# Edge ordering by source in a four-layer graph network: one of three scaled one-hots made on VectorE instead of ScalarE

## The chip, the core and the metric

The kernel runs on one core of a Trainium2 chip. A core has TensorE (PE in the profile; PEld is its weight load), VectorE (DVE), ScalarE (ACT), GpSimd (POOL) and SyncE (SP), each with an instruction queue of its own that is worked off in order; queues wait for each other through semaphores. The metric is the device time of one execution in microseconds, the median of several runs.

## What is computed

The input is a graph of 6250 nodes with 256 features each and 100000 edges (src, dst), sorted by dst. Four graph layers follow one another, each with a residual and a layer norm:

```python
edge_index = jnp.stack([src, dst])
x = _layernorm(x + _L0_gnn_ref(x, edge_index, ...))       # mean of relu(layernorm(x)) over the edges, two matrices
x = _layernorm(x + _L1_gnn_ref(x, src, dst, ...))         # attention with 8 heads: queries at src, keys and values at dst
x = _layernorm(x + _L2_gnn_ref(x, edge_index, ...))       # two graph attention layers with 4 heads
x = _layernorm(x + _L3_gnn_ref(x, edge_index, ...))       # mean of x over the edges, three matrices
```

Layers 0, 2 and 3 sum over the edges of each dst, for which the edges come in order. Layer 1 sums over the edges of each src (`segment_sum(..., row)` with `row = src`), so the kernel must order the edges by source first:

```python
s = jnp.einsum('ehd,ehd->eh', q[row], k[col])
m = jax.ops.segment_max(s, row, num_segments=n)
p = jnp.exp(s - m[row])
denom = jax.ops.segment_sum(p, row, num_segments=n)
out = jax.ops.segment_sum((p / denom[row])[:, :, None] * v[col], row, num_segments=n)
```

## The kernel before

**Blocks and pieces.** The nodes lie in 50 blocks of 125. Each block has 16 chunks of 128 edges of its own, and ten blocks share 2 more chunks for what doesn't fit. A layer's pass goes over *pieces*: in layer 0, three pieces a block with 6, 6 and 4 chunks, 150 in all (numbered 0 to 149 in the prediction). A piece (`piece0`, L1659) gathers its rows from a table in HBM with one indirect DMA per chunk, issued by POOL (`gather`, L926, L927), into a tile of which there are four buffers; makes the one-hot of its keys on DVE (`one_hots`, L936, three buffers); and adds the rows to the block's sum on PE (`add_rows`, L995). After a block's last piece `finish0` (L1613) does the layer's dense part: the mean (L1620), transposes, products with w_l and w_r (`product`, L923), residual and norm (L1638, L1639, L882 to L893), then the products for layer 1's k, v and q (L1646, L1650, L1652) and the stores to kv_table and q_table on SP's queue.

**Ordering by source beside it.** `by_source` (L1341) runs beside layer 0. It is a generator that yields the cost of each step, and `beside` (L1685) hands out about 7.3 us of it per piece. It first finds for each edge its block and its place in the block (`lo`, the place modulo 128; `col`, the chunk and block). The edges lie as 125 rows by 800 columns. For each column `c` (the loop at L1513) it then makes `oh` (L1518), the one-hot of `col` over a window of chunks and blocks, and `o1` (L1520), the one-hot of `lo` over the 128 places, both on DVE in 16-bit form; scales `o1` per row by two parts of the edge's value, `oa` (L1522) and `ob` (L1524), on ACT; and adds the products of `oa` and `ob` with `oh` to an accumulator in PSUM (L1529). All 800 columns add to the same accumulator. For the columns whose window reaches the last block (`w1 == NC`, columns 600 to 799) there is a third scaled one-hot, `oc`, the places times the block's number plus one (`val_c`, L1491), which is multiplied with the last ten columns of `oh` (L1535): it tells for the shared chunks which block each edge belongs to. `oh` has four buffers, `o1`, `oa`, `ob` and `oc` three each. After the last column the accumulator is closed (L1539) and decoded on DVE (L1542 to L1570) to the lists by source: `idx_s`, `key_s`, and `idx_1` (L1570), the list for the first chunks of blocks 0 and 1.

**Layer 1.** The first eight chunks of blocks 0 and 1, 16 gathers in all, are taken from the first rows of kv_table with `idx_1` (L1813, L1814), before the whole table is there. All other gathers (L1816) wait for the last row of kv_table, which block 49's `finish0` writes.

**What sets the order.** The program is recorded piece by piece, and a scheduler then lays the instructions of each engine's queue in an order by its own estimate of what is ready when. A change of one instruction's engine so moves others too, on all queues, the gathers of POOL among them.

Of the kernel before, what the change touches and what calls it, by code (L numbers as in the profile page):

```python
# [11 lines left out]
AF = mybir.ActivationFunctionType  # L12
ALU = mybir.AluOpType
# [3 lines left out]
P = 128  # L17
# [638 lines left out]
def gnn_stack_kernel(ctx: ExitStack, tc: tile.TileContext, ins, out):  # L656
# [13 lines left out]
    nc = tc.nc  # L670
# [21 lines left out]
    EQ, NG = EP, 8  # L692
# [47 lines left out]
    with ExitStack() as fast:  # L740
# [600 lines left out]
        def by_source(pool, work, psum):  # L1341
# [131 lines left out]
            lo, col = place, ups[1].rearrange("p g q -> p (g q)")  # L1473
# [16 lines left out]
            val_c = ups[0].rearrange("p g q -> p (g q)")  # L1490
# [9 lines left out]
            iota_h = pool.tile([P, NC], F16, name="iota_h")  # L1500
# [12 lines left out]
            for c in range(EC):  # L1513
                at = slice(c, c + 1)
                w0, w1 = wide[c]
                n = w1 - w0
                oh = work.tile([EQ, WIDE], F16, name="oh", bufs=4)
                nc.vector.tensor_scalar(oh[:, :n], iota_h[:EQ, w0:w1], col[:, at], None, op0=ALU.is_equal)  # L1518
                o1 = work.tile([EQ, P], F16, name="o1", bufs=3)
                nc.vector.tensor_scalar(o1, iota_h[:EQ, :P], lo[:, at], None, op0=ALU.is_equal)  # L1520
                oa = work.tile([EQ, P], F16, name="oa", bufs=3)
                nc.scalar.activation(oa, o1, AF.Copy, scale=val_a[:, at])  # L1522
                ob = work.tile([EQ, P], BF16, name="ob", bufs=3)
                nc.scalar.activation(ob, o1, AF.Copy, scale=val_b[:, at])  # L1524
                for o in (oa, ob):
                    for k, (c0, c1) in enumerate(banks):
                        e0, e1 = max(c0, w0), min(c1, w1)
                        if e0 < e1:
                            nc.tensor.matmul(  # L1529
                                acc[:, k, e0 - c0 : e1 - c0], o, oh[:, e0 - w0 : e1 - w0], start=False, stop=False  # L1530
                            )
                if w1 == NC:
                    oc = work.tile([EQ, P], F16, name="oc", bufs=3)
                    nc.scalar.activation(oc, o1, AF.Copy, scale=val_c[:, at])
                    nc.tensor.matmul(of_block, oc, oh[:, NM - w0 : n], start=False, stop=False)  # L1535
                if c % 4 == 3:
                    yield 3.6
# [27 lines left out]
            for o, v, n in ((idx_s, low[:, :NM], CM), (far_s, low[:, NM:], SH)):  # L1565
                nc.vector.tensor_scalar(
                    o.rearrange("p b c -> p c b"), v.rearrange("p (c b) -> p c b", c=n), float(N - 1), 0.0,
                    op0=ALU.min, op1=ALU.max,
# [20 lines left out]
        with tc.tile_pool(name="f0", bufs=1) as pool, tc.tile_pool(name="f0w", bufs=2) as work, tc.tile_pool(  # L1589
# [9 lines left out]
            scale = (D // 8) ** -0.5  # L1599
# [59 lines left out]
            def piece0(b, c0, n):  # L1659
# [15 lines left out]
                if last:  # L1675
                    add_rows(sums[b], st[:, n:, :], gs, CM, SH, 1)
                    yield
                    yield from finish0(b)

            work_s = by_source(spool, swork, psum)  # L1680
            work_d = shared_by_target(psum)

# [394 lines left out]
        with tc.tile_pool(name="f3", bufs=1) as pool, tc.tile_pool(name="f3w", bufs=2) as work, tc.tile_pool(  # L2077
            name="f3g", bufs=5
        ) as gp, tc.tile_pool(name="f3p", bufs=1, space=bass.MemoryType.PSUM) as psum:
            iota_h = pool.tile([P, P], F16, name="iota_h3")  # L2080
# [179 lines left out]
```

## Time and profile before

| what | us |
|---|---|
| median of 4 runs | 5157.44 (5155.97 to 5160.06) |
| profiled execution | 5153.93 |
| its span | 5152.0 |
| first and last `oc` (L1534) start | 991.0 and 1212.2 |
| last gather of layer 0 starts | 1244.59 |
| first gather of layer 1 with idx_s starts | 1274.92 |

The profile is of one execution. A row of a group gives the line, engine, operation, output and inputs, shapes and count, then the busy time in us and the mean duration in ns, then the engine's idle time just before and what ended it. Neighbouring instructions of DVE and ACT overlap: what an operation costs its queue is the distance from its start to the start of the next, which is less than its duration. A row of a timeline gives start, duration, engine, line, and in brackets the idle time before and its releaser.

### The profile page before, as it was taken

The numbers are of one execution on the slowest core, as the hardware profiler recorded it, in microseconds if no ns is written. First come the engines' busy times: TensorE is split into PE (matmuls) and PEld (weight loads), VectorE is DVE, ScalarE is ACT, GpSimd is POOL, SyncE is SP. The second block draws the span as 40 slices with busy tenths as digits, with TensorE's granted clock in tenths as the row PEclk, the third lists the DMA queues.
The fourth block names the chain that finished last, engine by engine and source line by source line (L and its number), as shares of the span: only waits on it lengthen the run. The fifth ranks groups of instructions, "written<-read, shape, count | busy, mean of one in ns | idle before, by whom it ended". The sixth has DMA issues, their size and how long they took to land.

```text
span 5152.0 us, 84598 instructions
## 1 busy us (share of the span) xinstructions
PE 4245.1 (82%) x27926; PEld 3093.2 (60%) x27926; DVE 3531.3 (69%) x10485; ACT 2162.9 (42%) x6203; POOL 3770.6 (73%) x3889
## 2 busy tenths in 40 slices
PE   0467999987999999987887887877777777799997
PEld 0245667665676676665666666655655565456675
DVE  7576788766888888876666666657777777423434
ACT  4011898895344344433444444434444444211222
POOL 6677777776777777757777777767777777677776
PEclk9777999988999999998999999989889899899998
DMA  4556677666777777764444544444444444789975
GB/s 131 146 158 178 177 193 192 186 173 181 222 224 227 223 226 226 226 180 120 133 132 130 137 131 134 130 118 132 132 132 134 133 135 135 208 241 246 246 208 146
DMA packets 365012, 883.97 MB, mean 172 GB/s; under 512 B 83596, under 2 KB 181954, under 8 KB 364562
## 3 DMA queue, kind: packets, MB, share of 16 engines
q0 software_dynamic: 232032, 702.40, 49.7%
q1 hardware_dynamic: 132530, 176.06, 11.7%
q8 instruction: 222, 3.64, 0.3%
q14 instruction: 228, 1.87, 0.1%
HBM read 791.50 MB, written 86.63 MB: 170 GB/s over the span
## 4 chain that ended last, share of the span: by engine, by line
PE 33%; POOL 28%; issue 17%; DMA 12%; DVE 9%; ACT 2%; SPq 0%; DVEq 0%; POOLq 0%; ACTq 0%
POOL g L927 26%; PE ps L1846 7%; DMA g<-hs_table_f,idx_d 5%; PE ps L995 4%; PE qe L1826 4%; PE po L923 3%; PE pt L923 3%; PE d L2180 3%; PE acc L1529 3%; DMA g<-x_table_f,idx_d 2%; DMA g<-kv_table_f,idx_s 2%; DMA g<-h_table_f,idx_d 1%; DVE st L936 1%; DVE a_hot L1897 1%; DVE msg L1982 1%
## 5 line engine op out<-in xcount | busy, mean ns | idle before, releaser
L927 POOL DMA_INDIRECT g<-hs_table_f,idx_d x1600 | 1535.0, 959 | 487.4 <-issue 427.7
L927 POOL DMA_INDIRECT g<-h_table_f,idx_d x800 | 791.9, 990 | 296.3 <-issue 209.9
L2048 PE MATMUL ps<-msg,st 128*125 128x260 f32 x3200 | 898.1, 424 | 74.1 <-DVE msg L1982 52.1
L927 POOL DMA_INDIRECT g<-kv_table_f,idx_s x784 | 748.7, 955 | 250.2 <-issue 181.9
L995 PE MATMUL ps<-g,st 128*128 128x256 bf16 (+1 forms) x4032 | 640.7, 285 | 187.1 <-DMA g<-h_table_f,idx_d 88.5
L2048 PEld LDWEIGHTS ps<-msg,st 128*125 128x125 f32 x3200 | 639.5, 208 | 212.1 <-issue 50.4
L927 POOL DMA_INDIRECT g<-x_table_f,idx_d x544 | 515.8, 948 | 186.3 <-issue 152.9
L995 PEld LDWEIGHTS <-st 128*128 128x128 bf16 x4536 | 448.8, 102 | 282.7 <-issue 174.4
L1982 DVE TENSOR_TENSOR msg<-g,pp 128x1024 f32<-128x1024 f32 x400 | 484.8, 1212 | 19.3 <-ACT pp L1979 18.5
L1976 DVE TENSOR_TENSOR e<-g,pe 128x16 f32<-128x16 f32 x400 | 67.6, 169 | 578.2 <-DMA g<-hs_table_f,idx_d 405.2
L2015 PE MATMUL pe<-ad_parts,ts 125*128 125x4 bf16 x4800 | 177.9, 165 | 323.0 <-DVE e L1976 267.8
L936 DVE TENSOR_TENSOR st<-iota_p,key_d 128x500 f32<-128x500 f32 (+1 forms) x550 | 409.7, 745 | 49.2 <-PE ps L995 27.5
L2015 PEld LDWEIGHTS <-ts 125*128 125x128 bf16 x4800 | 177.4, 96 | 436.2 <-issue 333.9
L1846 PE MATMUL ps<-msg,st 128*125 128x264 f32 x1600 | 421.8, 401 | 2.5 <-DVE msg L1780 2.3
L1979 ACT ACTIVATE pp<-r 128x16 f32<-128x16 f32 (+1 forms) x410 | 76.7, 187 | 628.2 <-DVE r L1970 438.4
L948 ACT CAST ts<-tp 125x512 bf16<-125x512 f32 x400 | 230.6, 577 | 247.2 <-PE tp L946 239.6
L1522 ACT ACTIVATE oa<-o,blk 125x128 f16<-125x128 f16 x800 | 312.5, 391 | 38.8 <-PE acc L1529 27.9
L1829 DVE TENSOR_TENSOR prod<-g,qe 128x512 f32<-128x512 f32 x400 | 270.4, 682 | 79.3 <-PE qe L1826 45.6
L1826 PE MATMUL qe<-q,ts 125*128 125x256 bf16 x2400 | 319.6, 276 | 5.4 <-DMA q<-q_table_f 3.3
L1846 PEld LDWEIGHTS ps<-msg,st 128*125 128x125 f32 x1600 | 283.1, 189 | 63.8 <-ACT st_s L978 2.5
L1897 DVE TENSOR_SCALAR a_hot<-a_nodes,a_ends 128x500 f16<-128x500 f16 x950 | 319.0, 363 | 2.3 <-PE a_acc L1919 2.1
L1919 PE MATMUL a_acc<-a_hot,a_st 128*128 128x500 f16 x950 | 292.8, 400 | 30.3 <-ACT a_row L1906 21.1
(463 smaller groups left out, 8703.2 us busy)
## 6 DMA issues: line engine op xcount, KB each, us to landing
g<-hs_table_f,idx_d POOLq DMA_INDIRECT x1600
a_table_f<-a_row SPq DMA_DIRECT2D x50, 437.5 KB
cnt<-a_table_f SPq DMA_DIRECT2D x50, 437.5 KB
xs<-x_table_f SPq DMA_DIRECT2D x50, 336.0 KB
g<-h_table_f,idx_d POOLq DMA_INDIRECT x800
g<-kv_table_f,idx_s POOLq DMA_INDIRECT x784
hs_table_f<-hs SPq DMA_DIRECT2D x100, 115.5 KB
own<-hs_table_f SPq DMA_DIRECT2D x100, 115.5 KB
```

Source lines behind the costliest of these rows:

```text
L923: nc.tensor.matmul(ps, aT[:, k, :], w[:, k, :], start=(i == 0), stop=(i == n - 1))
L927: nc.gpsimd.indirect_dma_start(out=g, out_offset=None, in_=table, in_offset=bass.IndirectOffsetOnAxis(ap=idx, axis=0))
L936: nc.vector.tensor_tensor(st, iota_p[:, None, :w].to_broadcast([P, n, w]), key[:, :, None].to_broadcast([P, n, w]), op=ALU.is_equal,)
L995: nc.tensor.matmul(ps[:, :m], st[:, i, :], g[:, i, k * D : k * D + m], start=(c0 + i == 0 and k == 2), stop=(c0 + i == CH - 1 and k == 0),)
L1522: nc.scalar.activation(oa, o1, AF.Copy, scale=val_a[:, at])
L1826: nc.tensor.matmul(qe[:, i, :], ts[:, i0 + i, :], q[:, k * D : (k + 1) * D], start=(k == 0), stop=(k == 2))
L1846: nc.tensor.matmul(sums[b], hot, m[:, i * H1 : (i + 1) * H1, :].rearrange("p h c -> p (h c)"), start=(c == 0), stop=(c == CH - 1),)
L1897: nc.vector.tensor_scalar(hots[k][:, i, :], nodes[:, r * RW : (r + 1) * RW], ends[:, s, c : c + 1], None, op0=ALU.is_equal,)
L1919: nc.tensor.matmul(accs[s, r], sts[s][:, c, :], hot[:, i, :], start=(c == reach[r][0]), stop=(c == reach[r][1] - 1),)
L1982: nc.vector.tensor_mul(msg[:, : n * H2, :C2].rearrange("p (n h) c -> p n h c", h=H2), g[:, :n, :D].rearrange("p n (h c) -> p n h c", h=H2) ...
L2015: nc.tensor.matmul(pe[:, i, :], ts[:, i, :], ad_parts[:, b, k, :], start=(k == 0), stop=(k == 2))
L2048: nc.tensor.matmul(sums[b][:B, : D + H2], hot, m[:, i * H2 : (i + 1) * H2, :].rearrange("p h c -> p (h c)"), start=False, stop=(c == CH - 1),)
```

## The change

In the columns whose window reaches the last block, the rows by place times the block are no longer made by an ACTIVATE from `o1` on ScalarE. A `tensor_scalar` on VectorE makes them from the same inputs as `o1` itself, in one operation of two parts: it compares the places 0 to 127 with `lo`, and multiplies the result with `val_c`. Both are scalars per row. The values of `oc`, its shape, its type and its three buffers stay, and so does the product that reads it.

```diff
@@ -1531,7 +1531,9 @@
                             )
                 if w1 == NC:
                     oc = work.tile([EQ, P], F16, name="oc", bufs=3)
-                    nc.scalar.activation(oc, o1, AF.Copy, scale=val_c[:, at])
+                    nc.vector.tensor_scalar(
+                        oc, iota_h[:EQ, :P], lo[:, at], val_c[:, at], op0=ALU.is_equal, op1=ALU.mult
+                    )
                     nc.tensor.matmul(of_block, oc, oh[:, NM - w0 : n], start=False, stop=False)
                 if c % 4 == 3:
                     yield 3.6
```

`oc` no longer depends on `o1`. In the changed kernel as built, DVE has 200 instructions more and ACT 200 fewer; the lines behind L1534 are two higher.

## The prediction

> **What bounds the kernel now.** I read the page first (which engine is busy when), then the busy time by stretches around the changed line, the waits and groups of that stretch, the chain of waits, and last the timelines of single engines. The page has no engine at its limit over the whole span:
>
> ```profile
> PE 4245.1 (82%) x27926; PEld 3093.2 (60%) x27926; DVE 3531.3 (69%) x10485; ACT 2162.9 (42%) x6203; POOL 3770.6 (73%) x3889
> ```
>
> The changed line runs only from 991.0 to 1212.2 us: 200 times, for columns 600 to 799 of the 800, where the window reaches the last block. Busy time by stretches (start:end, length, then busy us and count of PE, PEld, DVE, ACT, POOL, then clock, DMA share, GB/s):
>
> ```profile
> 650.00:950.00 300.00, 288.42 (x2499) 216.48 (x2499) 256.35 (x1062) 264.90 (x880) 227.49 (x239) 0.99 0.70 191
> 990.00:1050.00 60.00, 49.72 (x358) 35.64 (x356) 35.90 (x132) 43.89 (x147) 45.67 (x48) 0.91 0.65 174
> 1050.00:1100.00 50.00, 46.51 (x310) 32.18 (x308) 35.02 (x136) 48.77 (x165) 37.82 (x41) 0.90 0.68 188
> 1100.00:1150.00 50.00, 45.21 (x311) 32.09 (x310) 34.98 (x136) 47.20 (x159) 34.77 (x37) 0.91 0.61 167
> 1150.00:1215.00 65.00, 59.51 (x432) 44.03 (x431) 45.73 (x175) 60.79 (x202) 38.42 (x41) 0.91 0.54 149
> ```
>
> From 1050 on ACT is 94 to 98% busy and DVE 70%: ACT sets the pace. Who waits for it, from 990 to 1215 (total us, times, longest), and the changed group there:
>
> ```profile
> DVE oh L1518 <- PE acc L1535: 42.3, 60, 2.4
> ...
> POOL g L927 <- PE acc L1529: 23.2, 15, 5.9
> DVE o L1520 <- ACT oc L1534: 11.4, 37, 0.4
> ```
> ```profile
> L1534 ACT ACTIVATE oc<-o,ups 125x128 f16<-125x128 f16 x200 | 77.7, 389 | 1.4 <-PE acc L1535 1.4
> ```
>
> DVE waits 42 us for buffers that the `oc` product on PE frees. POOL, which issues the gathers (one per 1.25 us), has four long waits for PE (4.4, 5.9, 5.0 and 4.4 us at 1134, 1160, 1185 and 1209); beyond the usual 0.3 us they come to 18.7 us. The stage ends on POOL:
>
> ```profile
> 1209.64 0.94 POOL L927 DMA_INDIRECT g<-h_table_f,idx_d  x1 [4.41 <-PE acc L1529]
> ...
> 1244.59 0.95 POOL L927 DMA_INDIRECT g<-h_table_f,idx_d  x1 [0.30 <-issue]
> ...
> 1262.34 0.95 POOL L927 DMA_INDIRECT g<-kv_table_f,idx  x1 [0.31 <-issue]
> 1274.92 1.91 POOL L927 DMA_INDIRECT g<-kv_table_f,idx_s  x1 [11.64 <-DMA kv_table_f<-kv]
> ```
>
> The last gather of layer 0 starts at 1244.59; block 49 is then finished and written to kv_table, and the gathers of layer 1 that need all of that table start at 1274.92, 30.3 us later. The 14 early kv gathers between them (1245.84 to 1263.3) cost nothing: POOL would be idle. From 1300 the next stage is 99% PE-busy and unchanged, so a shift of 1274.92 goes into the end time one for one.
>
> **The change, part by part.**
>
> *ACT loses 200 ACTIVATEs.* Back to back they start 0.29 us apart (the `oa`, `ob`, `oc` rows of its timeline), so 58 us of ACT's 220 go. What is late next is the question, not these 58 us.
>
> *DVE gains 200 two-part operations.* No row has this form at 128 elements. The nearest are starts of neighbours on DVE (start, duration):
>
> ```profile
> 1108.57 0.26 DVE L1520 TENSOR_SCALAR o<-iota_h,place 125x128 f16<-125x128 f16 x1
> 1108.75 0.28 DVE L1518 TENSOR_SCALAR oh<-iota_h,ups 125x260 f16<-125x260 f16 x1
> ```
> ```profile
> 1356.05 0.27 DVE L859 TENSOR_SCALAR ln_t<-ln_y,ln_w 125x1 f32<-125x1 f32 x1
> 1356.24 0.42 DVE L1765 TENSOR_TENSOR x_sb<-x_sb,o 125x256 f32<-125x256 f32 x1
> ```
> ```profile
> 1359.88 0.14 DVE L850 TENSOR_SCALAR ln_w<-mv 125x1 f32<-125x1 f32 x1
> 1359.94 0.67 DVE L1829 TENSOR_TENSOR prod<-g,qe 128x512 f32<-128x512 f32 x1
> ```
>
> `o` is the same data with one scalar per row: 0.16 us unhindered, 0.205 mean over the stretch. L859 takes two scalars per row: 0.19 us with one element, against 0.06 for L850, which takes none. So `oc` is about 0.19 + 0.03 = 0.22 unhindered and 0.265 with the hindrance that `o` shows; I take 0.245, nearest to both. Ends: 0.15 (the second scalar free) and 0.33 (L859 plus 128 elements at the 1.1 ns each of L805, 2304 elements in 2.54 us). At 197 in the stretch: 48 us, from 30 to 65.
>
> [...]
>
> *DVE's sum.* In the changed kernel's built order, between DVE's 600th `oh` (990.2 us in the trace) and the last column operation stand 201 `oh`, 201 `o`, 197 `oc`, 23 one-hots L936 and 8 sets of finish0's operations. Mean starts apart where nothing waited: `oh` 0.236, `o` 0.205, L936 0.867, a set 3.83. Without `oc`: 47.4 + 41.2 + 19.9 + 30.6 = 139.1. The same prices give 145.5 for the order of before, where 220.4 us less 67.6 idle is 152.8, so I add 5%: 146.1. With `oc`: 194.4 us, and the columns end at 1184.6 if DVE never waits (before: 1210.6 for the last `o`). But a pacing engine does wait: ACT, which sets the pace now, idled 22.5 of 220 us (10%); DVE as a chaser idled 15% of 650:950. The others would have room: a block with 24 columns costs DVE 16.5 + 2.6 + 3.8 = 23 us, ACT 24 x 0.58 + some 3 = 17, POOL 20, and PE, which did a block in 20 us in 650:950 with four long products a column, has two and a short one here. So I take 6%, with ends 0 and 12%: columns end at **1197** (1185 to 1211).
>
> *The order on the other queues moves with it.* The scheduler thinks the columns done sooner. On PE the 800th column now comes before the last product of piece 139 of the 150 pieces (0 to 149); before, of piece 143. On POOL, 13 of the 16 early kv gathers now stand before the last four gathers of layer 0, against 2: 11 x 1.25 = 13.75 us that were hidden in the tail and now lie ahead of the last gather. SP's queue swaps some loads of h rows with stores of q rows near the end. Its issues take 0.3 to 0.4 us and it is idle between them, so I cost that at nothing; a load held behind a store would cost some 3 us (the landing of the last q store, 1276.4 to 1280.1).
>
> *POOL's sum.* The gather tiles have 4 buffers, so piece 143 can be gathered when PE is done with piece 139, some 2.5 us after the columns end. Then 36 h gathers and 13 kv gathers follow at 1.255: the last starts 60.2 us later, at 1197 + 2.5 + 60.2 = 1259.7, that is 15.1 later than 1244.59. The kv gathers themselves need idx_1, 15 to 20 us after the columns end, and POOL reaches them 25 us after: no wait, but little cover.
>
> *The tail.* Block 49 now has block 48's twelve products right behind its last gather's, with their input ready; before, they waited for x of block 48 and held block 49's w_l product to 8.2 us after the last L995. I take 5.2, so 3 us less (0 to 6). Net at the start of layer 1: 15.1 - 3 = **+12 us**.
>
> The three `oc` that move up to 452 us are 0.7 us where DVE waits for PE: nothing, at most 0.7.
>
> The profiled execution took 5153.9 us (span 5152.0 and 1.9 around it), 3.5 below the median of 5157.4. So 5166 for it, and 5169 against the median.
>
> **The rivals.**
>
> *A: ACT's relief wins (not slower).* Speaks for it: 54 us of DVE's waits (42.3 + 11.4) are for `oc` alone. If `oc` starts 0.15 apart, the columns end at 990.2 + 175.7 = 1166; POOL is then never held. It decides at 1177 (1239.7 - 62.7, where 1239.7 is 1244.59 - 18.7 + 13.75). Gain 18.7, cost 13.75, tail 3: -8 us, 5149. Against: L859's 0.19. [...]
>
> *B: DVE paces but hardly waits.* Columns end at 1180 to 1190: -5 to +5, about 5157. For: ACT and PE lose their own backlog. Against: 15% idle of DVE in 650:950.
>
> *C: DVE waits as it does now in 650:950, and more.* 12 to 15% idle, or `oc` at 0.33: columns end at 1211 to 1219, +26 to +34; a wait for idx_1 in front of the last h gathers would add up to 8. About 5187. POOL's gathers start 1.265 us apart among the 398 `o` and `oh` of the stretch and 1.25 apart without them (1245 to 1262), 2.5 us in all, so 197 more operations add 1.2. [...]
>
> That the instruction goes elsewhere than said is excluded: the build shows 200 more TensorScalar on DVE, 200 fewer on ACT.
>
> **How the numbers follow.** My case (columns end 1191 to 1205, +6 to +20, 5163 to 5177): 0.48. B: 0.20. A: 0.12. C: 0.20. A measurement of this kernel tells some 0.2% (10.3 us) from no change. Slower by more: 0.40 of my case and all of C, 0.60. Faster by more needs A and a tail at its best: 0.07. The rest, 0.33, is within. Range: A's lower half and C's upper half left out, 5151 to 5189.
>
> **What would show it.** Right: DVE 85 to 95% busy from 1000 to 1195 with ACT near 70%; the wait of `oh` for L1535 well under 42 us; `oc` at 0.28 to 0.35 us duration; last column `o` near 1197; last h_table gather near 1260; first idx_s gather near 1287. Wrong: `oc` as short as `o`; no POOL wait for PE between 1130 and 1200 (rival A); POOL waiting in front of a kv gather with h gathers behind it (C); or a stage after 1300 that changes length.

## The result and the profile after

The changed kernel takes 5149.31 us (median of 40 runs, 5141.96 to 5156.74), the kernel before 5157.2 in the same comparison (60 runs): a ratio of 0.9984, with a 95% interval of 0.9979 to 0.9988. The forecast was 5169; the time lies just below its range (5151 to 5189), and on the other side of no change. It is the number of rival A.

The profiled execution took 5160.14 us (span 5158.3), 10.8 above the median. The excess is not in the changed stretch. Before it, column 600 starts 7.3 us later than in the trace of before (996.43 against 989.17); behind it, from the first gather of layer 1 with idx_s to its end this execution has 5160.14 - 1272.83 = 3887.3 us, the one of before 5153.93 - 1274.92 = 3879.0, and those of the experiments below 3878.5 to 3883.8. No instruction of the change lies there, so I read the trace only up to that gather.

Busy time by stretches after the change (same columns as before: stretch, length, busy us and count of PE, PEld, DVE, ACT, POOL, clock, DMA share, GB/s):

```profile
990.00:1050.00 60.00, 58.73 (x484) 42.50 (x481) 56.79 (x252) 51.12 (x166) 45.36 (x49) 1.00 0.69 189
1050.00:1100.00 50.00, 47.07 (x356) 32.15 (x355) 47.62 (x213) 41.22 (x129) 38.11 (x40) 0.97 0.67 183
1100.00:1150.00 50.00, 48.94 (x390) 34.10 (x388) 49.59 (x228) 43.95 (x142) 38.11 (x40) 1.00 0.70 188
1150.00:1215.00 65.00, 57.73 (x373) 42.27 (x372) 47.06 (x171) 27.08 (x82) 49.45 (x52) 0.89 0.69 193
```

DVE is 95 to 99% busy where it was 70%, ACT 82 to 88% where it was 94 to 98%. DVE now sets the pace of the columns, as forecast; but POOL is not slowed: 40 gathers in each 50 us, one per 1.25 us. Who waits, from 990 to 1215 (total us, times, longest):

```profile
POOL g L927 <- issue: 47.6, 156, 0.3
PEld L1529 <- ACT ob L1524: 11.7, 49, 2.5
PEld L1529 <- ACT oa L1522: 10.8, 41, 0.5
...
DVE kv L1652 <- PE po L923: 9.2, 3, 6.6
```

DVE's 42.3 us of waiting for `oh`'s buffer (the product of `oc`, now L1537) and the 11.4 us of `o` for `oc` are gone. So are POOL's four long waits: only its usual 0.3 us per gather are left. The waits of PE for `oa` and `ob` are longer than before (22.5 against 17.7 us), but nothing that ends the stage hangs on them. The groups of DVE in the stretch and, from its timeline (start, duration), one column and the start of the next:

```profile
L1534 DVE TENSOR_SCALAR oc<-iota_h,place,ups 125x128 f16<-125x128 f16 x197 | 63.0, 320 | 2.8 <-PE acc L1537 2.6
L1520 DVE TENSOR_SCALAR o<-iota_h,place 125x128 f16<-125x128 f16 x211 | 59.4, 287 | 0.4 <-ACT ob L1524 0.2
```
```profile
1102.04 0.25 DVE L1520 TENSOR_SCALAR o<-iota_h,place 125x128 f16<-125x128 f16 x1
1102.21 0.30 DVE L1534 TENSOR_SCALAR oc<-iota_h,place,ups 125x128 f16<-125x128 f16 x1
1102.43 0.28 DVE L1518 TENSOR_SCALAR oh<-iota_h,ups 125x260 f16<-125x260 f16 x1
1102.63 0.50 DVE L1520 TENSOR_SCALAR o<-iota_h,place 125x128 f16<-125x128 f16 x1
```

From start to start, `o` takes 0.17 us here, `oc` 0.22, `oh` 0.20. The stretch begins with the first `oh` that is 310 wide, that of column 600 (the row counts two), and ends with the last `oc`; in the trace of before it ends with the last `o`. First the two rows of after, then those of before:

```profile
996.43 0.56 DVE L1518 TENSOR_SCALAR oh<-iota_h,ups 125x310 f16<-125x310 f16 x2
1170.00 0.30 DVE L1534 TENSOR_SCALAR oc<-iota_h,place,ups 125x128 f16<-125x128 f16 x1
```
```profile
989.17 0.55 DVE L1518 TENSOR_SCALAR oh<-iota_h,ups 125x310 f16<-125x310 f16 x2
1210.64 0.25 DVE L1520 TENSOR_SCALAR o<-iota_h,place 125x128 f16<-125x128 f16 x1
```

POOL's timeline at the end of the stage (start, duration, in brackets the idle time before and its releaser):

```profile
1212.47 0.95 POOL L927 DMA_INDIRECT g<-kv_table_f,idx  x1 [0.30 <-issue]
...
1242.54 0.95 POOL L927 DMA_INDIRECT g<-kv_table_f,idx  x1 [0.30 <-issue]
1243.79 0.95 POOL L927 DMA_INDIRECT g<-h_table_f,idx_d  x1 [0.31 <-issue]
...
1247.55 0.94 POOL L927 DMA_INDIRECT g<-h_table_f,idx_d  x1 [0.30 <-issue]
...
1272.83 1.91 POOL L927 DMA_INDIRECT g<-kv_table_f,idx_s  x1 [20.59 <-DMA kv_table_f<-kv]
```

Thirteen early kv gathers stand ahead of the last four h gathers, without a wait, and the last h gather starts at 1247.55, 3 us *later* than before, although the columns ended 40 us sooner. By these absolute times the gain at the start of layer 1 comes from the tail, which is 25.3 us against 30.3. Counted from column 600, which started 7.3 us later, the last h gather comes 4.3 us sooner than before, and the tail is 5.1 us shorter.

The whole stage moves by some microseconds from trace to trace: column 600 starts between 989.0 and 996.4 us in the nine of this study, and single traces do not tell whether that is the execution or the kernel. I therefore count from that start. All kernels by that measure, from timelines of DVE and POOL (us; of DVE's idle time, what the timeline lists):

| kernel | columns take | of it DVE idle | POOL held by PE | column 600 to first idx_s gather | against before | median against before |
|---|---|---|---|---|---|---|
| before | 221.5 | 68.5 | 4 long waits | 285.8 | | |
| after | 173.6 | 4.7 | no | 276.4 | -9.4 | -7.9 |
| early kv gathers last, after | 171.1 | 2.9 | no | 260.7 | -25.1 | -23.0 |
| early kv gathers last, before | 220.6 | 66.1 | 4 long waits | 283.2 | -2.6 | 0.0 |
| `oc` issued twice | 223.4 | 9.0 | 9 long waits | 313.7 | +27.9 | +27.2 |
| `oc` twice in two of three columns | 208.1 | 8.8 | 5 long waits | 300.4 | +14.7 | +12.7 |
| `oc` made once | 168.0 | 26.7 | no | 269.4 | -16.4 | -13.9 |
| `oc` with one scalar | 168.0 | 8.4 | no | 273.1 | -12.7 | -12.5 |
| more buffers, before | 220.2 | 67.8 | 4 long waits | 284.5 | -1.3 | +0.2 |

The last two columns agree within 3 us in every row: what the change does to the time is done by the start of layer 1, and that start is what has to be explained. Where POOL is not held, its own count of gathers gives it: take 1.25 us off for each early kv gather that stands ahead of the last four h gathers (13, 0, 8 and 11 in these four kernels, by POOL's timelines), and 276.4, 260.7, 269.4 and 273.1 all become 259.3 to 260.7, although DVE had between 141 and 169 us of work in the columns.

### The profile page after: what moved, and what is told of

Same layout as the page of the kernel before. It is cut to its first block, busy times and chain, and to the rows that moved or that the text cites. A ratio compares the mean times of both kernels' runs of the same rounds, so it can differ in the third digit from the quotient of the medians.

```text
span 5158.3 us, 84506 instructions
## 1 busy us (share of the span) xinstructions
PE 4225.4 (82%) x27926; PEld 3077.5 (60%) x27926; DVE 3560.2 (69%) x10685; ACT 2113.7 (41%) x6003; POOL 3783.3 (73%) x3889
## 5 line engine op out<-in xcount | busy, mean ns | idle before, releaser
L995 PE MATMUL ps<-g,st 128*128 128x256 bf16 (+1 forms) x4032 | 640.9, 284 | 220.3 <-DMA g<-h_table_f,idx_d 114.7
L995 PEld LDWEIGHTS <-st 128*128 128x128 bf16 x4536 | 449.0, 101 | 321.7 <-issue 212.9
L936 DVE TENSOR_TENSOR st<-iota_p,key_d 128x500 f32<-128x500 f32 (+1 forms) x550 | 409.4, 744 | 50.7 <-PE ps L995 30.7
L1522 ACT ACTIVATE oa<-o,blk 125x128 f16<-125x128 f16 x800 | 313.3, 392 | 46.8 <-PE acc L1529 27.3
```

Of the source, the lines that this page charges most:

```text
L936: nc.vector.tensor_tensor(st, iota_p[:, None, :w].to_broadcast([P, n, w]), key[:, :, None].to_broadcast([P, n, w]), op=ALU.is_equal,)
L995: nc.tensor.matmul(ps[:, :m], st[:, i, :], g[:, i, k * D : k * D + m], start=(c0 + i == 0 and k == 2), stop=(c0 + i == CH - 1 and k == 0),)
```

## The experiments

The theory after the result: DVE's sum was too large, so that the columns end before POOL is ever held; from there on POOL's own count of gathers sets the end, and the kv gathers that moved ahead eat most of the gain. The rival theory: the columns' end still sets the time, or the moved kv gathers are hidden.

**The early kv gathers behind the last h gather.** The order of POOL alone is changed: a gather with `idx_1` may be issued only after the last gather of layer 0.

```diff
-                    gather(g[:, i, :], h_table[:, :], idx_d[:, b, c0 + i : c0 + i + 1])
+                    last_g[0] = gather(g[:, i, :], h_table[:, :], idx_d[:, b, c0 + i : c0 + i + 1])
...
-                        gather(g[:, i, :], kv_table[:ROWS, :], idx_1[:, b, c0 + i : c0 + i + 1])
+                        with tc.issue_after(last_g[0].ins):
+                            gather(g[:, i, :], kv_table[:ROWS, :], idx_1[:, b, c0 + i : c0 + i + 1])
```

> The changed kernel, with its 16 early kv gathers queued on POOL behind the last gather of layer 0 (13 of them stood in front of the last four); the order of the other engines is the changed kernel's. Theory 1 (POOL's issue rate ends layer 0 once the columns end early enough): the last h_table gather starts 13 x 1.25 = 16 us earlier against the first one's start of the stretch, the 16 kv gathers (20 us) fit into the 25 us tail behind it, and the first idx_s gather comes 11 to 16 us earlier: about 5149 - 14 = 5135, ratio 0.9957 to the kernel before (0.995 to 0.997). Theory 2 (the dense products of the last blocks on PE end layer 0): the place of the kv gathers is of no account, 5149, ratio 0.9984.

Measured: 5135.06 us (5 runs), a ratio of 0.995 with an interval of 0.9936 to 0.9963 to the kernel before (5158.07). POOL's timeline of this kernel:

```profile
1229.40 0.95 POOL L927 DMA_INDIRECT g<-h_table_f,idx_d  x1 [0.30 <-issue]
1230.65 0.94 POOL L927 DMA_INDIRECT g<-kv_table_f,idx  x1 [0.30 <-issue]
...
1249.39 0.95 POOL L927 DMA_INDIRECT g<-kv_table_f,idx  x1 [0.30 <-issue]
1255.19 1.36 POOL L927 DMA_INDIRECT g<-kv_table_f,idx_s  x1 [4.85 <-DMA kv_table_f<-kv]
```

All sixteen kv gathers now lie in the tail, where POOL would be idle (20.59 us of waiting have become 4.85), and the last h gather starts 18.15 us sooner than after the change: thirteen gathers at 1.25 are 16.25, and the stage started 1.9 sooner. So the moved gathers did cost what they were priced at. This version is faster than both kernels.

The same edit in the kernel before, where only two of these gathers stood ahead of the last four h gathers:

> The kernel before with the same edit: only two kv gathers move behind the last h_table gather. Theory 1: 2 x 1.25 = 2.5 us less at most, 5154.7, ratio 0.9995, POOL still held by PE for some 19 us between 1130 and 1210. Theory 2: no change, 1.000. Together with the run of the changed kernel it prices ScalarE against VectorE with POOL's order the same in both: theory 1 says 16 to 20 us between them, theory 2 some 8.

Measured: 5158.03 us (11 runs), a ratio of 1.000 (0.9991 to 1.0009). POOL is still held by PE (waits of 4.3 to 5.8 us), and nothing is gained; but here only two gathers could move, 2.5 us at most, which this interval does not tell from nothing. In the changed kernel thirteen moved, for 14 us. With POOL's order the same in both, `oc` on VectorE instead of ScalarE is worth 23 us (5158.0 against 5135.1), more than the 16 to 20 that were expected: most of what the change can give was hidden by the order.

**`oc` issued twice.** In every column the same operation into the same tile a second time.

```diff
+                    nc.vector.tensor_scalar(
+                        oc, iota_h[:EQ, :P], lo[:, at], val_c[:, at], op0=ALU.is_equal, op1=ALU.mult
+                    )
```

> The changed kernel with the new operation issued twice for each column. If DVE's load decides whether POOL is held (theory 1), the columns end 197 x 0.225 = 44 us later than 1170, at 1214, POOL waits for PE and for idx_1, and the end comes 30 to 42 us after the changed kernel's: 5180 to 5191, ratio 1.004 to 1.007. If DVE has room to spare (theory 3: what counts is only that ACT is relieved), the time stays within 5 us of 5149.

Measured: 5185.31 us (4 runs), 1.0056 (1.0041 to 1.0072), inside what the first theory gave. 393 operations take 87.5 us on DVE, 0.223 each from start to start, and the columns 223.4 us. PE holds POOL again, nine times for 1.3 to 6.3 us.

**`oc` made once and used for all columns** (the shared chunks' sums by block are left out by this; the products on PE stay).

```diff
-                    oc = work.tile([EQ, P], F16, name="oc", bufs=3)
+                    if c == EC - 2 * GQ:
+                        oc = pool.tile([EQ, P], F16, name="oc_once")
```

> The changed kernel with oc made for the first of its columns alone and used for all (the sums for the shared chunks' blocks are so wrong; all other work stays). DVE is rid of the 44 us. Theory 1: POOL was not held in the changed kernel either, so nothing is won but the five kv gathers that this build leaves behind the last four h_table gathers (8 ahead, against 13): 6 us, 5143, ratio 0.997. Theory 4 (DVE's new load still costs part of the gain): 5133 or less, ratio under 0.9955.

Measured: 5144.16 us (7 runs), 0.9969 (0.9958 to 0.998). Without 196 of the operations, some 44 us of DVE's work, the time is only 5 us below the changed kernel's, and of these 5 all can come from the order: eight kv gathers instead of thirteen stand ahead of the last four h gathers (5 x 1.25 = 6.25). So the removal of the work itself gained nothing that can be seen: in the changed kernel DVE no longer sets the end. The columns themselves take only 5.6 us less, because DVE now waits 26.7 us for others.

**One scalar instead of two** (the block's number is left out of `oc`).

```diff
-                    nc.vector.tensor_scalar(
-                        oc, iota_h[:EQ, :P], lo[:, at], val_c[:, at], op0=ALU.is_equal, op1=ALU.mult
-                    )
+                    nc.vector.tensor_scalar(oc, iota_h[:EQ, :P], lo[:, at], None, op0=ALU.is_equal)
```

> The changed kernel with `oc` made by the comparison alone, without the multiplication by the second scalar (so the shared chunks' block numbers are not computed). It prices the second scalar. Theory 1 (each scalar per row costs about 0.06 us on DVE): `oc` takes a step of 0.16 to 0.17 where nothing waits, as `o` does, against 0.225 with two; DVE has 12 us less in the stretch. Since POOL is not held in the changed kernel, only the order of the kv gathers counts for the end (11 ahead of the last four h gathers instead of 13: 2.5 us), so 5145 to 5149. Theory 2 (the second scalar is free, 0.225 is what any operation made without a neighbour's overlap takes): the step stays above 0.20. Theory 3 (DVE still sets the end in the changed kernel): 12 us go, 5137.

Measured: 5145.14 us (10 runs), 0.9975 (0.9965 to 0.9985). From DVE's timeline of this kernel:

```profile
1102.19 0.26 DVE L1520 TENSOR_SCALAR o<-iota_h,place 125x128 f16<-125x128 f16 x1
1102.35 0.24 DVE L1534 TENSOR_SCALAR oc<-iota_h,place 125x128 f16<-125x128 f16 x1
1102.52 0.28 DVE L1518 TENSOR_SCALAR oh<-iota_h,ups 125x260 f16<-125x260 f16 x1
```

`oc` takes 0.168 us from start to start (mean of 196), about as `o` does, against 0.225 with two scalars: the difference is 0.06 us. The run leaves out the second scalar and the second operation (the product) together. The trace of before tells them apart at one element: L850, two operations with constants, takes 0.063 us (mean of 81 without idle time before or behind them), L859, two operations with two scalars per row, 0.185 (mean of 264). So it is the scalars that cost, if 128 elements behave as one does. Of DVE's 12 us, 4 arrived at the end, 2.5 of which the order explains (11 kv gathers ahead instead of 13); the rest is within the intervals of the two kernels.

**The columns' end put where the forecast had it.** `oc` is issued a second time in two of three columns.

```diff
+                    if c % 3 != 0:
+                        nc.vector.tensor_scalar(
+                            oc, iota_h[:EQ, :P], lo[:, at], val_c[:, at], op0=ALU.is_equal, op1=ALU.mult
+                        )
```

> The changed kernel with `oc` issued a second time in two of three columns: 132 operations more, 132 x 0.223 = 29 us more on DVE in columns 600 to 799. The columns so end near 1170 + 29 = 1199, less some 3 us for the start of the stretch, 1196: where the prediction saw them (1197). All 16 early kv gathers stand before the last ten gathers of layer 0. Theory 1 (only the sum for DVE was wrong; POOL's sum and the tail hold once the columns end there): POOL waits for PE again, and the last gather of layer 0 starts 2.5 + (36 + 16) x 1.255 = 67.8 us after the columns end, at 1264; with the tail 3 us shorter than before that is +16 us against before, 5174. Theory 2 (POOL's sum or the tail was wrong too): the last gather starts within 55 us of the columns' end, or the time is below 5163.

Measured: 5170.33 us (10 runs), 1.0025 (1.0015 to 1.0034). The columns end at 1199.2. POOL's waits for PE from 990 to 1215, and its timeline at the end:

```profile
POOL g L927 <- PE acc L1541: 24.7, 11, 6.6
```
```profile
1266.54 0.95 POOL L927 DMA_INDIRECT g<-h_table_f,idx_d  x1 [0.30 <-issue]
1291.55 1.90 POOL L927 DMA_INDIRECT g<-kv_table_f,idx_s  x1 [24.06 <-DMA kv_table_f<-kv]
```

The last h gather starts 67.3 us after the columns' end (67.8 expected: 2.5, then 52 gathers at 1.255), and the tail is 25.0 us. With its column end made real, the rest of the forecast's working gives the time to within 4 us, 2.3 of which are the tail (27.3 by the forecast). The first theory holds in its numbers: of the forecast's terms, the column end alone was far off. One step of POOL's sum met its number in another way, though. POOL's last long wait ends at 1193.84, before the columns do, and is for the buffer of piece 142 (42 h gathers follow from there). The first gather of piece 143 starts at 1201.41, 2.2 us after the columns' end and near the 2.5 of the sum, but without a long wait: POOL came to it by its own pace.

**More buffers in the kernel before.** Was 0.205 us a price of `o`, or did it hold waits for buffers?

```diff
-                oh = work.tile([EQ, WIDE], F16, name="oh", bufs=4)
+                oh = work.tile([EQ, WIDE], F16, name="oh", bufs=5)
...
-                o1 = work.tile([EQ, P], F16, name="o1", bufs=3)
+                o1 = work.tile([EQ, P], F16, name="o1", bufs=6)
```

> The kernel before with five buffers for `oh` instead of four and six for `o1` instead of three. Theory 1 (the 0.205 us of `o` in the trace of before holds short waits for buffers that ACT and PE free, no work of DVE): with more buffers `o` comes nearer to its 0.16, or the waits move to fewer and longer ones; since ACT sets the pace there, the columns end where they did, within 3 us of 1210, and the time stays 5157 within 6. Theory 2 (0.205 is DVE's own price, hindered by other engines): `o` stays at 0.20. Theory 3 (the buffers, not ACT, set the pace of before): the columns end more than 10 us earlier.

Measured: 5157.91 us in one run. DVE's waits from 990 to 1215:

```profile
DVE oh L1518 <- PE acc L1535: 44.3, 63, 1.9
DVE o L1520 <- ACT oc L1534: 10.8, 36, 0.6
```

They are what they were (42.3 and 11.4), the columns end at 1210.0, and `o` still has a mean of 0.199 (0.204 before). The buffers do not set the pace of before, which excludes the third theory of this run. Between the other two the run does not decide, since the waits did not go away. The kernels in which DVE hardly waits speak for the first: `o` takes 0.163 to 0.173 in all five of them (after, kv gathers last, twice, twice in two of three, one scalar), and 0.199 to 0.208 in all four in which it waits 26 us or more. The trace of before itself decides. Of its 140 `o` in the stretch that no listed wait follows, the 95 with no idle time before or behind them take 0.165 us, as in the changed kernel, and with ScalarE as busy as ever beside them; the other 45 take 0.29.

## Why the prediction was wrong

The step that failed is the sum for DVE: "With `oc`: 194.4 us", and the 6% of waiting on top, "columns end at **1197**". The columns took 173.6 us instead of 206.8. By term, from DVE's timeline after the change (start to start, listed waits taken out):

| term | prediction | measured | difference |
|---|---|---|---|
| `oh` | 47.4 | 44.3 | -3.1 |
| `o` | 41.2 | 33.2 | -8.0 |
| one-hots L936 | 19.9 | 20.0 | +0.1 |
| the rest, finish0 above all | 30.6 | 26.9 | -3.7 |
| the 5% | 7.0 | 0 | -7.0 |
| `oc` | 48 | 44.4 | -3.6 |
| waiting | 12.4 | 4.7 | -7.7 |

Five terms and the waiting lean the same way, and for the operations of the columns, where the steps can be counted one by one, for one reason: they are means over a stretch in which DVE waited, with only the *listed* waits taken out (of the 3.1 us of `oh` this explains about half: those without idle time around them take 0.228 before and 0.219 after). The trace of before shows what was left in (start, duration, idle before):

```profile
1105.17 0.30 DVE L1518 TENSOR_SCALAR oh<-iota_h,ups 125x310 f16<-125x310 f16 x1 [0.99 <-PE acc L1535]
1105.39 0.40 DVE L1520 TENSOR_SCALAR o<-iota_h,place 125x128 f16<-125x128 f16 x1
1105.92 0.30 DVE L1518 TENSOR_SCALAR oh<-iota_h,ups 125x310 f16<-125x310 f16 x1
...
1111.04 0.25 DVE L1520 TENSOR_SCALAR o<-iota_h,place 125x128 f16<-125x128 f16 x1
1111.20 0.28 DVE L1518 TENSOR_SCALAR oh<-iota_h,ups 125x260 f16<-125x260 f16 x1
```

The `o` at 1105.39 ends at 1105.79, and the next operation starts at 1105.92: a gap of 0.13 us that no row lists (rows list only gaps above 0.15). By starts it makes an `o` of 0.53. At 1111.04, where DVE worked without a gap, `o` takes 0.16. Moreover, an `o` that itself came out of a listed wait took 0.241 to a next start that followed without a gap (26 of them). The prediction saw the 0.16, named it "unhindered", called the 0.205 "hindrance" and carried it over to `oc`. But the hindrance was waiting, and when DVE became the bound its idle time in the columns fell from 68.5 to 4.7 us. The 5% were the same thing once more: they fitted the prices to a stretch that had waits in it. There an operation in front of a listed wait counts with its whole duration, since no neighbour overlaps it: 0.255 us for 58 of the 198 `o`. That the excess comes from waits, and is not a price that other engines' work imposes, is shown by the 95 `o` at 0.165 in the same trace, and by the five kernels at 0.163 to 0.173, which have more work on DVE, not less.

The 6% for waiting came from two other engines, ACT as the pacer and DVE as a chaser. DVE as the pacer waited 2.7%. One reading was off too: the 600th `oh` starts at 988.41 in the trace, and the 990.2 taken for it is the start of the 603rd (the 601st and 602nd stand merged in one row). These 1.8 us are small beside the 33 that the columns' length was off.

Point by point:

- *ACT's 200 operations* were taken off a path that they set. That DVE would set the pace next was right: its stretches are 95 to 99% full. The lower end of the range for the columns, 1185, was still 15 us too late.
- *The price of `oc`.* "about 0.19 + 0.03 = 0.22 unhindered" was right (0.225 mean, 0.223 median), and the row that it came from, L859 with two scalars and one element, was the nearest. The 0.245 taken was too high, and again by the "hindrance". The runs show 0.168 us with one scalar per row and 0.225 with two.
- *POOL's sum* held: the gathers from 1000 to 1160 start 1.27 us apart in the mean beside 95 to 99% of VectorE work (median 1.25), against 1.26 before (median 1.25; the 4.1 us beyond the usual 0.3 of the long wait at 1134 taken out), and the run with the forecast's column end has the last gather within 3 us of where the working puts it. The 0.01 us more per gather leave no room for a wait of POOL of 0.22 us, the step of an `oc`, at each of the 197 operations.
- *The moved kv gathers*: 1.25 us each was right, as the run with late kv gathers and the kernels with 8 and 11 of them ahead show; so 11 x 1.25 = 13.75.
- *The tail*: 3 us shorter was forecast, with ends 0 and 6; it was 5.1 shorter after the change, and 24.4 to 26.1 us in the other kernels with `oc` on DVE or made once, against 30.3 and 31.1 in the two of before that were measured first, and 27.5 in the one with more buffers. The reason given for it is to be seen on PE: block 49's w_l product starts 4.3 us after the end of the last L995 product (1257.73 and 1253.40), where 5.2 was forecast and 8.2 was measured before, and block 48's twelve products stand ahead of it with their input ready.
- *What was costed at nothing* (SP's swapped loads and stores, the three `oc` moved up): nothing in the trace speaks for a cost; the wait at 1272.83 is for the last kv rows, as before.
- *The rivals.* A had the right mechanism, and sizes close to the measured ones: the columns end before 1177 (1170), POOL is never held, -18.7 + 13.75 - 3 = -8 us. It got its column end, 1166, from an `oc` of 0.15, which is not what `oc` takes, on top of the same high prices for the rest: 175.7 us for the columns, against 173.6 measured, is two errors that cancel, and so luck. With `oc` at 0.225 and the other terms as measured the columns are done as early. The sign of the time did not hang on `oc`'s price but on which prices were used for the operations already there. Its chance, 0.12, was too low: a single condition, columns done by 1177, stood 20 us from the value taken, and nearly all terms of that value were on the high side.

## What to carry to other kernels

Price the work of an engine that is to become the bound from stretches in which it worked back to back (here 0.16 us for `o`), not from means over a stretch in which it waited: short waits are not listed, and an `o` that came out of a wait took longer (0.241 us against 0.165), so both are counted as work, and a percentage that makes the sum fit such a stretch adds more of the same. When an engine stops holding a queue, look at the order of that queue next: here 13.75 of the 18.7 us gained were given back by gathers that the scheduler moved ahead, and putting them back behind was worth more than the change itself (5135 against 5149 us; the change gave 8). Without the change there was nothing to gain there but two gathers. Where a floor lies near (POOL's gathers at 1.25 us each), work out the point at which it is reached and how far the forecast's terms are from it; past it the rest of the saving is lost, as the run without the operation shows.

## What the runs showed of the hardware

- The `tensor_scalar` of `oc` on VectorE, at 128 elements of 16 bits, took 0.168 us with one scalar per row and one operation, 0.221 to 0.227 with two and two (start to start, in the kernels in which DVE hardly waits). In the trace of before, with one element and two operations, no such scalar took 0.063 (L850) and two took 0.185 (L859). About 0.06 us for each scalar is an estimate from these four numbers.
- An `o` on VectorE that had just come out of a wait took longer: 0.241 us from its start to the next (26 cases in the trace of before, with no gap behind them), against 0.165 in an unbroken row of operations (95 cases).
- PE's granted clock was 0.97 to 1.00 from 990 to 1150 after the change and 0.90 to 0.91 before, with PE 94 to 98% busy against 83 to 93%. In the run with `oc` twice in two of three columns, in which PE holds POOL as it does before, the clock was 0.91 to 0.95. What the clock follows from no run here tells. The columns' pace is not explained by it: in that run DVE idles only 8.8 us, at the low clock.
